# Experts of two routed layers: blocks of 256 slots, two experts' weights per turn, 20 turns in place of 23

## The chip, the cores and the metric

One Trainium2 chip, one core of it. The metric is the device time of one execution in microseconds (us). The kernel is one program for a whole small network: four layers, each an attention and a feed-forward part.

## The reference, cut to what matters

`x` is 32 x 128 tokens of 128 features. Two of the four feed-forward parts are mixtures of 8 experts. Every token goes to its 2 best experts and gets their weighted sum back. Cut to what the change touches:

```python
# layer 1, feed-forward: E = 8 experts, K = 2, hidden F = 256
gate = jnp.sum(jax.nn.one_hot(idx, E) * w[..., None], axis=1)      # 2 of 8 are not zero
hid = jax.nn.silu(jnp.einsum('td,edf->tef', t, w1)) * jnp.einsum('td,edf->tef', t, w3)
y = jnp.einsum('ted,te->td', jnp.einsum('tef,efd->ted', hid, w2), gate)
# layer 2, feed-forward: E = 8, K = 2, hidden DF = 512
h = jax.nn.gelu(jnp.einsum('td,efd->tef', xf, W1) + b1, approximate=False)
y = jnp.einsum('tef,edf->ted', h, W2) + b2
out = jnp.einsum('ted,te->td', y, w)
```

The other parts (three attentions, a scan-like one, two dense feed-forwards) are computed before, between and after, and the change does not edit them.

## The kernel before, in words

The program runs in stages. Layers 0 and 1 share one long stage. Then come the experts of layer 1 (**stage f1**), the attention of layer 2, the experts of layer 2 (**stage f2**), and a tail for layer 3.

`Routes` (L672 on) holds the routing of one mixture. Each token's row is stored twice, once for each of its experts, into a room in DRAM (`self.room`, name `by_expert_r`), by GpSimd's indirect DMAs (L699). The room is cut into blocks of `slots` rows; `LOTS` (L29) says 512. Each expert owns the blocks of its full capacity (4,096 rows), but only its first block is always computed. What overflows is found at run time: `tables` (L772) counts the tokens of each expert and lists the further blocks that hold tokens. `_room` (L63) gives the number of blocks that must be computed so that every token is covered whatever the routing: 8 first blocks and `more` = 15 listed ones, 23 in all. The blocks are zeroed during layer 0, four blocks to a DMA (`clear`, L686, issued at L998 by `cleared`).

`Routes.run` (L804) computes the blocks, one a **turn**:

- `load` (L824): SyncE (SP) issues two DMAs, the expert's weights into `w` (three buffers) and the block's 512 rows into `xt` (three buffers). For the 8 first blocks both addresses are fixed ("static"). For the listed ones SP first reads two registers from the table (L814, "dynamic"). The DMAs of SP are issued in the order in which they stand in its queue, and each waits there until its buffer is free.
- `first` (L841): TensorE turns the rows (four 128x128 transposes into `tpe`), ScalarE or VectorE moves them to `xT`, and `hidden` makes the hidden layer. That is `swiglu` (L1198) in f1: for each of 2 slices of 128 hidden features a matmul with w1 and one with w3 (L1203, L1205), Silu on ScalarE, a product on VectorE. In f2 it is `gelu` (L1378): for each of 4 slices one matmul (L1382) and one Gelu with a bias column of the expert (L1385).
- `second` (L847): 2 (f1) or 4 (f2) accumulating matmuls with w2 (L851) and `finish`, a ScalarE move to `yT` (L1212; L1389 with the bias b2).
- `third` (L856): four transposes back, a VectorE copy to `yt` (L858), and one DMA that stores the block over its old place (L859).

Turns are software pipelined: at turn i the loop at L868 records the load of block i+2, `first` of i+1, `third` of i-1 and `second` of i. A scheduler then orders each engine's instructions by its own estimate, so transposes of the next block and matmuls of the last one interleave. Every f32 matmul is two instructions on TensorE, each with a weight load of its own (PEld), which overlaps the instruction before it.

In f1, GpSimd also clears the key and query stacks of layer 2's attention (L355, L357), and SP loads the first of its keys (L401, 288 KB each) between the block DMAs. After each expert stage the next one gathers the rows back with indirect DMAs (L886).

Of the kernel before, what the change touches and what calls it, by code (L numbers as in the profile page):

```python
# [12 lines left out]
F32 = mybir.dt.float32  # L13
# [3 lines left out]
AF = mybir.ActivationFunctionType  # L17
# [5 lines left out]
P = 128  # L23
NB = 4
E = 8
D = 128
EPS = 1e-5

LOTS = dict(r1=(0, 8, 512), r2=(0, 8, 512))  # L29
MAGIC = 12582912.0  # L30


# [25 lines left out]
E1 = _Cols(w1=256, w3=256, w2=256)  # L58
E2 = _Cols(w1=512, w2=512, b1=4, b2=1)
# [3 lines left out]
def _room(lot):  # L63


    first, end, slots = LOTS[lot]
    cap = (end - first) * NB * P
    more = (2 * cap - E) // slots
    return cap, more, E * cap // slots + more + 1


@with_exitstack
def tile_flamingo_gated(
# [20 lines left out]
    nc = tc.nc  # L94
# [190 lines left out]
    def flat(a):  # L285
        return a.rearrange("p b s -> p (b s)")
# [85 lines left out]
    class Stacks:  # L372
# [13 lines left out]
        def load(self, n, parts, at, group):  # L386

            t = self.slots[n].take()
            heads = slice(0, 9 * self.d)
            for e in range(self.halves):  # L390
                dst = t[heads, 4 * e : 4 * (e + 1)]
                if n == 0:
                    first = (self.H * e + 4 * at) * NB * P
                    src = parts.rearrange("d c h n -> (d c) (h n)")[:, first : first + 4 * NB * P]
                    nc.sync.dma_start(
                        out=dst.rearrange("p m b k -> p (m b k)"),
                        in_=src[:, None, :].to_broadcast([3 * self.d, 3, 4 * NB * P]),
                    )
                else:
                    src = parts.rearrange("(h e) d a (c n) -> e (d a c) h n", e=self.halves, n=NB * P)[e]  # L400
                    nc.sync.dma_start(  # L401
                        out=dst.rearrange("p m b k -> p m (b k)"), in_=src[:, 4 * at : 4 * (at + 1)]
                    )
            if n and self.bias:
                rows = bias_rows[self.bias][:, group * NB * P : (group + 1) * NB * P]
                nc.sync.dma_start(
                    out=t[72:75, 0:4].rearrange("p m b k -> p m (b k)"),
                    in_=rows[:, None, :].to_broadcast([3, 4, NB * P]),
                )
            return t  # L410
# [261 lines left out]
    class Routes:  # L672
# [131 lines left out]
        def run(self, pool, psum, weights, cols, turned, hidden, n_f, finish, spare=1):  # L804

            def static(i):
                block = i * (self.cap // self.slots)
                return slice(block, block + 1), slice(i, i + 1)  # L810

            def dynamic(i):
                vals = [
                    nc.values_load(  # L814
                        table[0:1, k, i : i + 1], engines=[mybir.EngineType.SP], min_val=0, max_val=top,
                        skip_runtime_bounds_check_because="bounded where the table is made",
                    )
                    for k, top in ((1, self.blocks - 1), (0, E - 1))
                ]
                return bass.ds(vals[0], 1), bass.ds(vals[1], 1)  # L820

            n_c = self.slots // P

            def load(i):  # L824
                block, e = static(i) if i < E else dynamic(i - E)
                w = pool.tile([P, cols.n], F32, tag="w", name="w", bufs=3)
                nc.sync.dma_start(out=w, in_=weights[e].rearrange("o p n -> (o p) n"))
                xt = pool.tile([P, n_c, D], F32, tag="xt", name="xt", bufs=2 + spare)
                ins = nc.sync.dma_start(
                    out=xt.rearrange("p c d -> p (c d)"), in_=self.room[block].rearrange("o p n -> (o p) n")  # L830
                )
                self.apart(ins, "tiles", "no two tiles share a block")
                return block, w, xt

            def turn(a):
                tp = psum.tile([P, n_c, P], F32, tag="tp", name="tpe")
                for c in range(n_c):
                    nc.tensor.transpose(tp[:, c, :], a[:, c, :], ident)  # L838
                return tp

            def first(i):  # L841
                block, w, xt = loaded.pop(i)
                xT = pool.tile([P, self.slots], F32, tag="xT", name="xT")
                turned(xT, flat(turn(xt)))
                return block, w, hidden(w, xT)

            def second(block, w, hid):  # L847
                y = psum.tile([P, self.slots], F32, tag="y", name="ye")
                w2 = cols(w, "w2").rearrange("p (f d) -> p f d", d=D)
                for f in range(n_f):  # L850
                    nc.tensor.matmul(y, lhsT=w2[:, f, :], rhs=hid[:, f, :], start=f == 0, stop=f == n_f - 1)  # L851
                yT = pool.tile([P, n_c, P], F32, tag="yT", name="yT", bufs=1 + spare)
                finish(flat(yT), w, y)
                return block, yT

            def third(block, yT):  # L856
                yt = pool.tile([P, n_c, D], F32, tag="yt", name="yt")
                nc.vector.tensor_copy(yt, turn(yT))  # L858
                ins = nc.sync.dma_start(out=self.room[block].rearrange("o p n -> (o p) n"), in_=flat(yt))  # L859
                self.apart(ins, "tiles", "no two tiles share a block")  # L860

            n = E + self.more
            loaded = {0: load(0), 1: load(1)}
            yield
            hid, done = first(0), None
            table = self.tables(pool, psum)
            yield
            for i in range(n):  # L868
                if i + 2 < n:
                    loaded[i + 2] = load(i + 2)  # L870
                after = first(i + 1) if i + 1 < n else None
                if done:
                    third(*done)
                done = second(*hid)
                hid = after
                yield
            third(*done)
            self.done = True

# [308 lines left out]
    with ExitStack() as outer:  # L1188
# [3 lines left out]
        with ExitStack() as stack:  # L1192
            pool, psum = mlp_pools(stack, "f1")

            def turned(xT, tp):
                nc.scalar.mul(xT, tp, COL(col, "g2"))

            def swiglu(w, xT):  # L1198
                hid = pool.tile([P, 2, 512], F32, tag="hid", name="hid", bufs=3)
                for f in range(2):  # L1200
                    fs = slice(f * P, (f + 1) * P)
                    p1 = psum.tile([P, 512], F32, tag="h", name="p1", bufs=3)
                    nc.tensor.matmul(p1, lhsT=E1(w, "w1")[:, fs], rhs=xT, start=True, stop=True)  # L1203
                    p3 = psum.tile([P, 512], F32, tag="h", name="p3", bufs=3)
                    nc.tensor.matmul(p3, lhsT=E1(w, "w3")[:, fs], rhs=xT, start=True, stop=True)  # L1205
                    sil = pool.tile([P, 512], F32, tag="sil", name="sil", bufs=3)
                    nc.scalar.activation(sil, p1, AF.Silu)
                    nc.vector.tensor_tensor(hid[:, f, :], p3, sil, ALU.mult)  # L1208
                return hid

            def finish(yT, w, y):
                nc.scalar.copy(yT, y)  # L1212

            for _ in routes1.run(pool, psum, e1_d, E1, turned, swiglu, 2, finish):
                pass
# [156 lines left out]
        with ExitStack() as stack:  # L1372
            pool, psum = mlp_pools(stack, "f2")

            def turned(xT, tp):
                nc.vector.tensor_scalar(xT, tp, COL(col, "gamma"), COL(col, "beta"), ALU.mult, ALU.add)

            def gelu(w, xT):  # L1378
                hid = pool.tile([P, 4, 512], F32, tag="hid", name="hid", bufs=3)
                for f in range(4):  # L1380
                    ph = psum.tile([P, 512], F32, tag="h", name="ph", bufs=3)
                    nc.tensor.matmul(  # L1382
                        ph, lhsT=E2(w, "w1")[:, f * P : (f + 1) * P], rhs=xT, start=True, stop=True
                    )
                    nc.scalar.activation(hid[:, f, :], ph, AF.Gelu, bias=E2(w, "b1")[:, f : f + 1])  # L1385
                return hid

            def finish(yT, w, y):
                nc.scalar.activation(yT, y, AF.Identity, bias=E2(w, "b2"))  # L1389

            for _ in routes2.run(pool, psum, e2_d, E2, turned, gelu, 4, finish):
                pass
# [236 lines left out]
```

## Time and profile before

| | us |
|---|---|
| median of 3 runs | 2178.75 (2176.64 to 2182.37) |
| the profiled execution, its own time | 2170.34 |
| its span, first to last instruction | 2168.5 |
| stage f1, first weight DMA issued to last store landed | 1261.0 to 1419.7 |
| stage f2, the same | 1781.3 to 1976.7 |
| TensorE busy over the span | 1658.0 (76%) |
| mean granted TensorE clock | 0.860 |
| moved by DMA | 244.66 MB, mean 113 GB/s |

How to read it. A row of a group reads: line, engine, operation, `out<-in`, shapes, count, then busy us and the mean ns of one, then the idle time of the engine ahead of it and who ended it. In the chain of waits each row is start, length and what. In the timeline "SPq" rows are DMAs being issued by SP, not the transfer. Matmuls are pipelined: a row "x2 1.02" is two instructions that overlap, so the spacing is read from start to start.

### The profile page before, as it was taken

The numbers are of one execution on the slowest core, as the hardware profiler recorded it, in microseconds if no ns is written. First come the engines' busy times: TensorE is split into PE (matmuls) and PEld (weight loads), VectorE is DVE, ScalarE is ACT, GpSimd is POOL, SyncE is SP. The second block draws the span as 40 slices with busy tenths as digits, with TensorE's granted clock in tenths as the row PEclk, the third lists the DMA queues.
The fourth block names the chain that finished last, engine by engine and source line by source line (L and its number), as shares of the span: only waits on it lengthen the run. The fifth ranks groups of instructions, "written<-read, shape, count | busy, mean of one in ns | idle before, by whom it ended". The sixth has DMA issues, their size and how long they took to land.

```text
span 2168.5 us, 35498 instructions
## 1 busy us (share of the span) xinstructions
PE 1658.0 (76%) x13624; PEld 1010.3 (47%) x13624; DVE 1197.4 (55%) x3504; ACT 894.0 (41%) x1110; POOL 638.6 (29%) x637
## 2 busy tenths in 40 slices
PE   0599998989999999878777569926666629995355
PEld 0455445456656666555455424414555514442223
DVE  7645446475545476766666433357667631113797
ACT  0376565565787745333323223301111204441244
POOL 5101101020000012454544482056443430003550
PEclk9999999999999999987877779966667759997566
DMA  6564558634332343112212035435344212332110
GB/s 214 154 230 154 187 184 266 219 101 124 105 100 67 94 145 84 51 54 59 56 48 55 25 116 174 141 104 148 110 124 121 71 63 101 135 132 86 41 49 20
DMA packets 164536, 244.66 MB, mean 113 GB/s; under 512 B 20560, under 2 KB 102288, under 8 KB 164112
## 3 DMA queue, kind: packets, MB, share of 16 engines
q1 hardware_dynamic: 156176, 225.62, 34.0%
q0 software_dynamic: 8192, 16.79, 2.7%
q8 instruction: 107, 1.75, 0.4%
q14 instruction: 61, 0.50, 0.1%
HBM read 139.74 MB, written 101.24 MB: 111 GB/s over the span
## 4 chain that ended last, share of the span: by engine, by line
PE 40%; DVE 14%; POOL 13%; issue 8%; ACT 2%; DMA 2%; SPq 0%; POOLq 0%; DVEq 0%; ACTq 0%
PE ye L851 5%; PE ph L1382 4%; PE av L644 4%; POOL by_expert_r L699 4%; PE sct L561 4%; POOL got L886 3%; PE sc L561 3%; PE ph L1037 3%; PE p L1203 2%; PE tpe L838 2%; DVE mx L592 2%; PE p L1205 2%; PE tp L282 1%; POOL r L208 1%; POOL w L249 1%
## 5 line engine op out<-in xcount | busy, mean ns | idle before, releaser
L627 ACT ACTIVATE w<-sct 128x1024 f32<-128x1024 f32 x288 | 292.8, 1024 | 346.4 <-PE sct L561 345.2
L592 DVE TENSOR_REDUCE mx<-sc 128x8 f32<-128x1024 f32 x160 | 194.9, 1220 | 130.0 <-PE sc L561 129.6
L561 PEld LDWEIGHTS <-stack_q 96*128 96x128 bf16 x2560 | 194.4, 110 | 134.5 <-issue 104.3
L886 POOL DMA_INDIRECT got<-by_expert_r,slot_r x128 | 127.7, 998 | 360.8 <-issue 335.0
L597 DVE TENSOR_REDUCE mx<-sc 128x4 f32<-128x1024 f32 x128 | 152.9, 1222 | 132.8 <-PE sc L561 132.3
L644 PE MATMUL av<-w,va 128*9 128x128 f32 (+2 forms) x3584 | 198.1, 295 | 36.7 <-POOL w L630 31.9
L561 PE MATMUL sc<-stack_k,stack_q 96*128 96x128 bf16 x1536 | 145.7, 244 | 46.8 <-DMA stack_k<-k 17.4
L561 PE MATMUL sct<-stack_q,stack_k 128*128 128x128 bf16 (+1 forms) x1536 | 139.5, 236 | 17.3 <-DVE mx L592 8.3
L561 PEld LDWEIGHTS <-stack_k 128*128 128x128 bf16 (+1 forms) x1536 | 111.8, 107 | 69.6 <-issue 66.6
L644 PEld LDWEIGHTS av<-w,va 128*9 128x9 f32 (+2 forms) x3584 | 98.6, 94 | 87.5 <-POOL w L630 43.5
L851 PE MATMUL ye<-hid,w 128*128 128x512 f32 x276 | 133.4, 593 | 2.3 <-DVE hid L1208 2.3
L311 POOL CAST hml<-whole 128x512 bf16<-128x512 f32 (+1 forms) x48 | 30.1, 626 | 343.0 <-ACT whole L310 166.7
L1037 PE MATMUL ph<-h,w 128*128 128x512 f32 x256 | 123.7, 610 | 1.8 <-ACT hn L1040 0.9
L1037 PE MATMUL ph<-hn,w 128*128 128x512 f32 x256 | 121.2, 604 | 0.7 <-ACT hn L1040 0.7
L208 POOL TENSOR_TENSOR r<-r,m 128x4 f32<-128x4 f32 x56 | 58.5, 1044 | 188.8 <-DVE r L207 175.0
L561 PE MATMUL sc<-stack_l,stack_q 96*128 96x128 bf16 x1024 | 110.4, 238 | 0.0
L650 ACT COPY ot<-av 128x512 f32<-128x512 f32 x112 | 65.5, 584 | 99.5 <-PE av L644 96.6
L630 POOL TENSOR_SCALAR_AFFINE_SELECT w<-w 128x1024 f32<-128x1024 f32 x64 | 70.8, 1106 | 113.9 <-ACT w L627 113.7
L561 PE MATMUL sct<-stack_q,stack_l 128*128 128x128 bf16 x1024 | 98.9, 234 | 2.7 <-DVE mx L592 2.7
L627 ACT ACT_TABLE_LOAD x72 | 92.4, 1283 | 9.7 <-PE sct L561 8.5
L699 POOL DMA_INDIRECT by_expert_r<-yn,slot_r x64 | 65.6, 1025 | 83.1 <-DVE slot_r L757 25.4
L656 PE MATMUL tpo<-cst,ot 128*128 128x128 f32 x448 | 82.4, 306 | 9.5 <-ACT ot L650 6.9
(295 smaller groups left out, 3290.5 us busy)
## 6 DMA issues: line engine op xcount, KB each, us to landing
by_expert_r<-zeros SPq DMA_DIRECT2D x40, 1024.0 KB
stack_q<-q SPq DMA_DIRECT2D x96, 288.0 KB
stack_k<-k SPq DMA_DIRECT2D x96, 288.0 KB
k<-hml SPq DMA_DIRECT2D x16, 1152.0 KB
w<-in_e_dram SPq DMA_DIRECT2D x23, 514.5 KB
xt<-by_expert_r SPq DMA_DIRECT2D x46, 256.0 KB
by_expert_r<-yt SPq DMA_DIRECT2D x46, 256.0 KB
q<-hml SPq DMA_DIRECT2D x72, 128.0 KB
```

The source lines that it names most:

```text
L208: nc.gpsimd.tensor_tensor(r, r, m05.to_broadcast([P, NB]), ALU.pow)
L561: nc.tensor.matmul(dst[:, h * P : (h + 1) * P], lhsT=stat[rows, 4 * e + h, b], rhs=mov[rows, 4 * e + h, b], start=start and h == e == 0, s ...
L592: latest["maxima"] = nc.vector.tensor_reduce(mx[:, :, b0 : b0 + 2].rearrange("p h b -> p b h"), sc.rearrange("p i (h k) -> p i h k", h=4), ...
L597: nc.vector.tensor_reduce(mx[:, :, b0], sc.rearrange("p i (h k) -> p h i k", h=4), AX.XY, ALU.max, negate=True,)
L627: latest["weights"] = nc.scalar.activation(w.rearrange("p i h k -> p i (h k)"), sc, AF.Exp)
L644: nc.tensor.matmul(av[32 * h : 32 * h + dv + 1, b * P : (b + 1) * P], lhsT=values[c][:, b, 4 * u + h, :], rhs=w[:, i, h, :], start=c == 0, ...
L656: nc.tensor.transpose(tp[:, b].rearrange("p s r -> p (s r)"), ot[:, b, :], ident)
L699: ins = nc.gpsimd.indirect_dma_start(out=self.rows(), out_offset=bass.IndirectOffsetOnAxis(ap=slots, axis=0), in_=rows, in_offset=None,)
L851: nc.tensor.matmul(y, lhsT=w2[:, f, :], rhs=hid[:, f, :], start=f == 0, stop=f == n_f - 1)
L886: ins = nc.gpsimd.indirect_dma_start(out=got[:, k, b, :], out_offset=None, in_=self.rows(), in_offset=bass.IndirectOffsetOnAxis(ap=self.sl ...
L1037: nc.tensor.matmul(ph, lhsT=wt[:, c, f * P : (f + 1) * P], rhs=h[:, c, :], start=c == 0, stop=c == 3)
L1382: nc.tensor.matmul(ph, lhsT=E2(w, "w1")[:, f * P : (f + 1) * P], rhs=xT, start=True, stop=True)
```

## The change

A block has 256 slots. A turn takes two blocks, the halves of the same 512 columns, each with the weights of its own expert. `_room` then gives `more` = 31, made 32 so that the sum is even: 40 blocks, 20 turns, and 161 blocks of 256 rows in each room in place of 80 of 512. In a turn, `load` issues four DMAs and up to four pairs of register reads, every 512-column matmul becomes two of 256 columns with different weights, `third` stores with two DMAs, and in f2 each Gelu and each move with b2 becomes two of 256 columns, since the bias differs. Silu, the products, the transposes, `xT` in both stages and the copy `yt` keep their shape. The zeroing of the rooms goes in pieces of 8 blocks of 1 KB rows.

```diff
-LOTS = dict(r1=(0, 8, 512), r2=(0, 8, 512))
+LOTS = dict(r1=(0, 8, 256), r2=(0, 8, 256))
+HALVES = slice(0, 256), slice(256, 512)
...
     more = (2 * cap - E) // slots
+    more += (E + more) % 2
     return cap, more, E * cap // slots + more + 1
...
-            def load(i):
-                block, e = static(i) if i < E else dynamic(i - E)
-                w = pool.tile([P, cols.n], F32, tag="w", name="w", bufs=3)
-                nc.sync.dma_start(out=w, in_=weights[e].rearrange("o p n -> (o p) n"))
-                xt = pool.tile([P, n_c, D], F32, tag="xt", name="xt", bufs=2 + spare)
-                ins = nc.sync.dma_start(
-                    out=xt.rearrange("p c d -> p (c d)"), in_=self.room[block].rearrange("o p n -> (o p) n")
-                )
-                self.apart(ins, "tiles", "no two tiles share a block")
-                return block, w, xt
+            def load(u):
+                w = pool.tile([P, 2, cols.n], F32, tag="w", name="w", bufs=3)
+                xt = pool.tile([P, 2 * n_c, D], F32, tag="xt", name="xt", bufs=2 + spare)
+                blocks = []
+                for half in range(2):
+                    i = 2 * u + half
+                    block, e = static(i) if i < E else dynamic(i - E)
+                    nc.sync.dma_start(out=w[:, half], in_=weights[e].rearrange("o p n -> (o p) n"))
+                    ins = nc.sync.dma_start(
+                        out=xt[:, half * n_c : (half + 1) * n_c].rearrange("p c d -> p (c d)"),
+                        in_=self.room[block].rearrange("o p n -> (o p) n"),
+                    )
+                    self.apart(ins, "tiles", "no two tiles share a block")
+                    blocks.append(block)
+                return blocks, [w[:, 0], w[:, 1]], xt
...
-                for f in range(n_f):
-                    nc.tensor.matmul(y, lhsT=w2[:, f, :], rhs=hid[:, f, :], start=f == 0, stop=f == n_f - 1)
+                for w, at in zip(ws, HALVES):
+                    w2 = cols(w, "w2").rearrange("p (f d) -> p f d", d=D)
+                    for f in range(n_f):
+                        nc.tensor.matmul(
+                            y[:, at], lhsT=w2[:, f, :], rhs=hid[:, f, at], start=f == 0, stop=f == n_f - 1
+                        )
...
-                ins = nc.sync.dma_start(out=self.room[block].rearrange("o p n -> (o p) n"), in_=flat(yt))
-                self.apart(ins, "tiles", "no two tiles share a block")
+                for half, block in enumerate(blocks):
+                    ins = nc.sync.dma_start(
+                        out=self.room[block].rearrange("o p n -> (o p) n"),
+                        in_=yt[:, half * n_c : (half + 1) * n_c].rearrange("p c d -> p (c d)"),
+                    )
+                    self.apart(ins, "tiles", "no two tiles share a block")
...
-            n = E + self.more
+            n = (E + self.more) // 2
...
                     p1 = psum.tile([P, 512], F32, tag="h", name="p1", bufs=3)
-                    nc.tensor.matmul(p1, lhsT=E1(w, "w1")[:, fs], rhs=xT, start=True, stop=True)
                     p3 = psum.tile([P, 512], F32, tag="h", name="p3", bufs=3)
-                    nc.tensor.matmul(p3, lhsT=E1(w, "w3")[:, fs], rhs=xT, start=True, stop=True)
+                    for p, name in ((p1, "w1"), (p3, "w3")):
+                        for w, at in zip(ws, HALVES):
+                            nc.tensor.matmul(p[:, at], lhsT=E1(w, name)[:, fs], rhs=xT[:, at], start=True, stop=True)
...
-                    nc.tensor.matmul(
-                        ph, lhsT=E2(w, "w1")[:, f * P : (f + 1) * P], rhs=xT, start=True, stop=True
-                    )
-                    nc.scalar.activation(hid[:, f, :], ph, AF.Gelu, bias=E2(w, "b1")[:, f : f + 1])
+                    for w, at in zip(ws, HALVES):
+                        nc.tensor.matmul(
+                            ph[:, at], lhsT=E2(w, "w1")[:, f * P : (f + 1) * P], rhs=xT[:, at], start=True, stop=True
+                        )
+                    for w, at in zip(ws, HALVES):
+                        nc.scalar.activation(hid[:, f, at], ph[:, at], AF.Gelu, bias=E2(w, "b1")[:, f : f + 1])
...
-            def finish(yT, w, y):
-                nc.scalar.activation(yT, y, AF.Identity, bias=E2(w, "b2"))
+            def finish(yT, ws, y):
+                for w, at in zip(ws, HALVES):
+                    nc.scalar.activation(yT[:, at], y[:, at], AF.Identity, bias=E2(w, "b2"))
```

More of the change, by code (lines that the diff above doesn't have):

```diff
@@ L835, in turn, with first @@
             def turn(a):
-                tp = psum.tile([P, n_c, P], F32, tag="tp", name="tpe")
-                for c in range(n_c):
+                tp = psum.tile([P, 2 * n_c, P], F32, tag="tp", name="tpe")
+                for c in range(2 * n_c):
                     nc.tensor.transpose(tp[:, c, :], a[:, c, :], ident)
                 return tp
-            def first(i):
-                block, w, xt = loaded.pop(i)
-                xT = pool.tile([P, self.slots], F32, tag="xT", name="xT")
+            def first(u):
+                blocks, ws, xt = loaded.pop(u)
+                xT = pool.tile([P, 2 * self.slots], F32, tag="xT", name="xT")
@@ L844, in first @@
                 turned(xT, flat(turn(xt)))
[L845 to L849, printed above, removed]
-                for f in range(n_f):
[L851 to L854, printed above, removed]
@@ L856, in third, with second @@
-            def third(block, yT):
-                yt = pool.tile([P, n_c, D], F32, tag="yt", name="yt")
-                nc.vector.tensor_copy(yt, turn(yT))
-                ins = nc.sync.dma_start(out=self.room[block].rearrange("o p n -> (o p) n"), in_=flat(yt))
-                self.apart(ins, "tiles", "no two tiles share a block")
-            n = E + self.more
+                return blocks, ws, hidden(ws, xT)
+            def second(blocks, ws, hid):
+                y = psum.tile([P, 2 * self.slots], F32, tag="y", name="ye")
+                for w, at in zip(ws, HALVES):
[4 more added lines that the diff above has]
+                        )
+                yT = pool.tile([P, 2 * n_c, P], F32, tag="yT", name="yT", bufs=1 + spare)
+                finish(flat(yT), ws, y)
+                return blocks, yT
@@ new lines, in third @@
+            def third(blocks, yT):
+                yt = pool.tile([P, 2 * n_c, D], F32, tag="yt", name="yt")
+                nc.vector.tensor_copy(yt, turn(yT))
+                for half, block in enumerate(blocks):
[4 more added lines that the diff above has]
+                    self.apart(ins, "tiles", "no two tiles share a block")
@@ L1196, in turned, with swiglu @@
                 nc.scalar.mul(xT, tp, COL(col, "g2"))
-            def swiglu(w, xT):
+            def swiglu(ws, xT):
                 hid = pool.tile([P, 2, 512], F32, tag="hid", name="hid", bufs=3)
@@ L1376, in turned, with gelu @@
                 nc.vector.tensor_scalar(xT, tp, COL(col, "gamma"), COL(col, "beta"), ALU.mult, ALU.add)
-            def gelu(w, xT):
+            def gelu(ws, xT):
                 hid = pool.tile([P, 4, 512], F32, tag="hid", name="hid", bufs=3)
@@ L1381, in gelu, with finish @@
                     ph = psum.tile([P, 512], F32, tag="h", name="ph", bufs=3)
-                    nc.tensor.matmul(
-                        ph, lhsT=E2(w, "w1")[:, f * P : (f + 1) * P], rhs=xT, start=True, stop=True
-                    )
-                    nc.scalar.activation(hid[:, f, :], ph, AF.Gelu, bias=E2(w, "b1")[:, f : f + 1])
-                return hid
-            def finish(yT, w, y):
-                nc.scalar.activation(yT, y, AF.Identity, bias=E2(w, "b2"))
+                    for w, at in zip(ws, HALVES):
[4 more added lines that the diff above has]
+                        nc.scalar.activation(hid[:, f, at], ph[:, at], AF.Gelu, bias=E2(w, "b1")[:, f : f + 1])
+                return hid
+            def finish(yT, ws, y):
+                for w, at in zip(ws, HALVES):
+                    nc.scalar.activation(yT[:, at], y[:, at], AF.Identity, bias=E2(w, "b2"))
             for _ in routes2.run(pool, psum, e2_d, E2, turned, gelu, 4, finish):
```

## The prediction

> **What bounds the kernel now.** I read the chain of waits first, cut to the two expert stages. In f1 and in f2 it repeats with the turn (start, length, what):
>
> ```profile
> 1320.77 1.04 PE p L1203 x2
> 1321.81 0.86 PE p L1205 x2
> 1322.67 0.86 PE p L1203 x2
> 1323.53 0.86 PE p L1205 x2
> 1324.38 0.44 PE tpe L838 x4
> 1324.82 0.86 PE ye L851 x2
> 1325.68 0.44 PE tpe L838 x4
> 1326.12 0.86 PE ye L851 x2
> ...
> 1858.54 3.63 PE ph L1382 x8
> 1862.50 2.58 PE ye L851 x6
> 1865.52 0.86 PE ye L851 x2
> 1866.49 3.63 PE ph L1382 x8
> ```
>
> Only TensorE stands in it. The f2 turn is 1866.49 - 1858.54 = 7.95 us; the f1 turn, from the first p to the next turn's (1326.98 to 1333.24), 6.26 us. Then the table by stretches, one inside each stage (length, PE, PEld, DVE, ACT and POOL busy, granted clock, DMA share, GB/s):
>
> ```profile
> 1320.00:1340.00 20.00, 20.00 (x63) 9.23 (x62) 5.94 (x9) 7.74 (x13) 0.00 (x0) 1.00 0.52 151
> 1860.00:1880.00 20.00, 20.00 (x62) 9.45 (x61) 3.69 (x5) 9.26 (x14) 0.00 (x0) 1.00 0.38 131
> ```
>
> TensorE is busy all the time at the full clock, every other engine under half, the DMA engines 0.52 and 0.38. So a turn is worth its TensorE time, as long as its rows and weights arrive. Of the span, 23 x 6.26 = 144.0 and 23 x 7.95 = 182.9 us are turns.
>
> **TensorE, turn by turn.** An instruction of 512 columns has one weight load (PEld, 190 ns) and starts every 0.43 us: 3.17 us for seven, less the 0.592 us of one, over six gaps. For 256 columns there is no row. From below it takes half, 0.215 us. From above, the nearest row with a load per instruction, in layer 1's projection:
>
> ```profile
> 532.39 0.89 PE L1099 MATMUL po<-wa,oT 128*128 128x128 f32 x6
> 533.12 3.17 PE L1037 MATMUL ph<-h,w 128*128 128x512 f32 x7
> ```
>
> Six of 128 columns in 0.73 us are 0.122 us each, where a quarter of 0.43 is 0.107: the load shows 0.015 us at most. At 256 columns the stream is longer than the load's 0.19 us, so I take 0.216. A turn of f1 then has 24 x 0.216 = 5.18 us of matmuls in place of 12 x 0.43 = 5.16, one of f2 32 x 0.216 = 6.91 in place of 16 x 0.43 = 6.88; the eight transposes stay. A turn hardly grows, and three go: -18.8 in f1, -23.9 in f2, +1.0 for the longer matmuls of 40 turns (+8.4 at 0.015 a piece).
>
> The Trainium skill, "TensorE: Matmul & The Clock Gate", section Back-to-back issue gap, speaks against this: it gives a sustained spacing of 81 ns at 128 columns and 131 ns at 512 and says that both the load and the matmul set it. By it, halving the columns would not halve the time. Row L1099 does not agree for f32 here: a quarter of the columns took 0.28 of the time. An estimate from the page's two figures, 98 ns at 256 columns by a straight line, would make the matmuls of a turn half as long again, 2.6 us more in f1 and 3.4 in f2, and end near 2262. As a mechanism of this kernel it is rival D.
>
> **Fillers.** In f1 the matmuls wait for xT: transposes 0.44 and ScalarE 0.69 us (L1196), with one ye (0.86) in between and a gap of 0.13 us. In the built program's order one half ye and three transposes stand there (0.75 us): +0.1 us a turn, +2 in all; in some turns the four transposes are split and the gap shrinks, so I take +1. In f2 `finish` becomes two moves. A 512-column one took 0.687 us (L1389); the Silu rows of 512 and 1024 columns (0.598, 1.024) give 0.83 ns a column, so 256 columns take 0.47 and the pair 0.95. In the built order the transposes of yT come 0.86 us after the last ye (rows, 0.43, and half a ye, 0.43) and now wait for about 1.2: +0.16 us a turn. The gap ahead of ph (0.10) is filled by more work: -0.10. In all +0.06 x 20 = +1.2. The eight Gelus of a turn take 8 x 0.47 = 3.8 us in place of 2.75, beside 7.9 us of TensorE; the bank of the first is free 0.5 us before the fourth ph wants it, so they stay hidden. If that cover went, each f2 turn would pay up to 1.0.
>
> **Loads.** This is where the change adds: a turn fetches 2 x 384 + 256 KB in f1 (2 x 514.5 + 256 in f2) in place of 384 + 256, with four DMAs, and stores with two. All stand in SP's queue; w waits there until the turn three before is finished, and everything behind it waits too. Two turns of that queue:
>
> ```profile
> 1363.29 0.33 SPq L827 DMA_DIRECT2D w<-in_e_dram  x1
> 1363.87 0.36 SPq L859 DMA_DIRECT2D by_expert_r<-yt  x1
> 1364.75 0.33 SPq L829 DMA_DIRECT2D xt<-by_expert_r  x1
> ...
> 1865.89 0.33 SPq L827 DMA_DIRECT2D w<-in_e_dram  x1
> 1866.72 0.33 SPq L829 DMA_DIRECT2D xt<-by_expert_r  x1
> ```
>
> A dynamic load costs SP 0.83 to 0.88 us (register reads included), a store 0.58. SP is then busy 4 x 0.85 + 2 x 0.58 = 4.6 us a turn, under 6.26. The arrival matters more. The DMA rows of 1363 to 1371 us, in slices of 0.2 us:
>
> ```profile
> DMA  0000002699477999977977510000000000000359
> GB/s 0 0 0 0 0 0 61 169 261 200 184 215 302 364 358 369 394 287 266 297 287 276 215 62 20 0 0 0 0 0 0 0 0 0 0 0 0 46 61 154
> ```
>
> Data flow 0.9 us after the issue, and weights, store and rows (0.92 MB) are through in 3.3 us: 280 GB/s. In f1 after the change, counted from the end of a turn's last ye, the four issues are at 0.2, 1.05, 1.9 and 2.75 us; 1.05 MB at 280 GB/s from 1.1 on end at 4.9. Those rows are wanted after the next turn's transposes, ye, yT, p and ye, 6.0 to 6.2 us. Slack 1.2 us. In f2 the weights come free 1.2 us after the last ye (the later `finish`), 1.31 MB end at 1.2 + 0.9 + 4.7 = 6.8, wanted at 8. So both stay hidden. In f1 four of the eight key loads (288 KB, 1.05 us each at that rate) stand in the built order between later turns' fetches and eat the slack, the others behind the last fetch: 0 to 1 us for each of four turns; I take +1.0, less the 0.9 us that a late xt cost TensorE before (1319.28, next to key loads), so +0.1.
>
> Starts and ends: the first turn needs both halves, 1.05 MB in place of 0.66 MB: +1.2 us a stage, +2.4. The last store is two issues (+0.58 us) of half the bytes (-0.4): +0.4 in all. The table's three operations grow from 120 to 256 elements, +0.1 us each beside TensorE: 0.
>
> Zeroing: 42 DMAs in place of 40, rows of 1 KB in place of 2. No row shows that store; from below 0, from above the rate falls from 340 GB/s to the 290 of the 512-byte loads at 7 to 11 us, 21 us of DMA time for 41 MB. It lies in layer 0, where TensorE is busy 37 of 40 us and the DMA engines 0.5 to 0.8 (140 to 420 us): 0. The scheduler also reorders some of layers 0 and 1: 0 +- 4.
>
> **Sum.** -18.8 - 23.9 + 1.0 + 1.0 + 1.2 + 0.1 + 2.4 + 0.4 = -36.6. The profiled execution took 2170.34 us, span 2168.5 and 1.8 around it: 2134. It was 8.4 us under the median of the runs shown, so the forecast is 2178.75 - 36.6 = 2142.
>
> **The rivals.**
>
> - A, the forecast: 2134 to 2152 (the ends: fillers and starts free and layers 0 and 1 four us better; or +8.4 for the loads on TensorE and the Gelus half hidden).
> - B, f1 becomes bound by transfers. If a row costs the same whether it is 1 or 2 KB (384 rows in 3.3 us now, 768 then), a turn's DMA takes 6.6 us, with a key load 7.6: twenty turns are 136 us, -8 in place of -17: 2151; 7.1 us a turn would make it 2161. For it: the DMA share is 0.52 already. Against: the kernel's first loads, in rows of 512 bytes, run at 290 GB/s. F2 keeps its gain (6.6 under 7.9).
> - C, slower: SP becomes the bound. The first dynamic fetch came 1.88 us after its store (1312.25 to 1314.13). At that price SP needs 4 x 1.88 + 2 x 0.58 = 8.7 us for a turn, more than TensorE in both stages. Sixteen of the twenty turns are dynamic: 16 x 8.7 + 4 x 6.3 = 164 in f1, 16 x 8.7 + 4 x 8 = 171 in f2, +20 and -12, and +3 for starts: 2190. It decides from 1.79 us a fetch on. Against: every later fetch shows 0.85.
> - D, slower: weight loads are not hidden behind 256 columns. A turn has 12 (f1) or 16 (f2) more of them, 560 in all. Wholly exposed they cost 560 x 0.19 = 106 us: 2178.75 - 37.6 + 106 = 2247. It ends slower than before from 0.067 us a load on. Against: 0.015 in row L1099.
> - E, layers 0 and 1 pay for the zeroing or the new order, 5 to 15 us of the 21: about 2152.
>
> **How the numbers follow.** A 0.67, B 0.14, E 0.09, C 0.05, D 0.05. Faster by over 0.3% (6.5 us, about what a measurement of this kernel can tell from no change): A, B and E, 0.90. Within: 0.03 of C, at fetches a little under its price. Slower: D and 0.02 of C, 0.07. The range takes A, B and E and leaves C and D out: 2134 to 2162.
>
> **What would show it.** In the profile after: spacing of 256-column matmuls 0.216 us (D: 0.28 or more); TensorE busy 20 of 20 us and clock 1.00 inside both stages; turns of 6.2 to 6.4 and 7.9 to 8.0 us; f1 some 16 us shorter, f2 some 21; xt as releaser of the transposes only in the first turn and beside the key loads (B, C: in every dynamic turn); DMA share near 0.7 in f1 and 0.6 in f2; layer 2's attention starting 15 to 18 us earlier and all before 1255 us unmoved (E). I am wrong if the rows arrive later than 6.2 us after a turn's last ye in f1, if a dynamic fetch costs SP much more than 0.85 us, or if a load costs TensorE more than 0.067 us.

## The result, and the profile after

The changed kernel takes 2145.0 us, the kernel before 2177.7 in the same comparison: a ratio of 0.985 (95% interval 0.983 to 0.987), 33 us less where 36.6 were forecast. A second comparison, in which both were some 10 us shorter, gave 2133.5 and 2167.8, ratio 0.984 (0.981 to 0.987). The forecast of 2142, its direction and its range held. Not all of its terms did: f1 gained 5 us less than forecast, f2 2 us more. Of the four executions of e7 below, one took 2537.3 us at a mean granted clock of 0.627 where the others have 0.859 to 0.861; no ratio uses it, and without it e7's median is 2124.5.

The stages, from two profiles of each kernel (us). f1 and f2 begin with their first fetch; f1 ends with the next stage's first load, which SP issues behind the last store, and f2 with the issue of its last store.

| | f1 begins | f1 | attention of layer 2 | f2 | tail | span |
|---|---|---|---|---|---|---|
| before | 1261.0 | 158.9 | 361.3 | 193.7 | 193.5 | 2168.5 |
| before, second profile | 1257.9 | 158.8 | 361.5 | 193.8 | 193.3 | 2165.4 |
| after | 1258.8 | 148.1 | 371.9 | 172.0 | 191.7 | 2142.5 |
| after, second profile | 1257.8 | 148.0 | 362.0 | 170.8 | 192.7 | 2131.3 |

Between the two second profiles the 34.1 us lie in f1 (-10.8) and f2 (-23.0), and the rest is -0.3. Of the 10 us that the first profile of after has too much in the attention, 8.2 are one wait, told below (e5).

First the stretches that were shown of before, now of after (length, PE, PEld, DVE, ACT and POOL busy, granted clock, DMA share, GB/s):

```profile
1320.00:1340.00 20.00, 18.72 (x94) 15.39 (x94) 6.04 (x9) 7.21 (x12) 0.00 (x0) 1.00 0.63 190
1860.00:1880.00 20.00, 19.80 (x100) 16.86 (x99) 3.00 (x4) 10.46 (x26) 0.00 (x0) 1.00 0.65 204
```

TensorE is no longer busy all of the 20 us: it lacks 1.3 in f1 and 0.2 in f2. The clock is 1.00 as before, so the throttle has no part in it. The chain of waits of after shows who took the 1.3 us; an f1 turn, then an f2 turn (start, length, what):

```profile
1345.67 0.69 DVE yt L869
1346.37 0.02 issue
1346.38 0.35 SPq L871
...
1346.94 0.36 SPq L871
1347.29 0.04 issue
1347.34 0.27 SPq L817
...
1347.86 0.35 SPq L834
...
1348.76 0.36 SPq L835
...
1349.97 0.34 SPq L834
...
1350.82 3.06 DMA xt<-by_expert_r
1353.88 0.04 issue
1353.93 0.44 PE tpe L846 x2
...
1355.14 3.72 PE p L1221 x16
...
1856.14 0.47 ACT yT L1408
1856.63 0.35 SPq L834
...
1859.17 4.72 DMA xt<-by_expert_r
1863.89 0.04 issue
1863.94 0.44 PE tpe L846 x2
...
1865.68 3.45 PE ph L1399 x16
1869.13 2.60 PE ye L860 x12
```

Before, only TensorE stood here. Now the chain of an f1 turn runs from the copy `yt` through SP's two stores (L871), the register reads (L817), the four fetches (w L834, xt L835) and the landing of the rows, and only then back to the transposes. In some turns of f2 it leaves TensorE too, as here: from the move to `yT`, the last reader of a weight buffer, through the four fetches to the rows. There it costs little; the 20 us of f2 lack 0.2. The same in the list of waits of after, over 1268 to 1400 us, so without the start of the stage (total us, times, longest):

```profile
PEld tpe L846 <- DMA xt<-by_expert_r: 9.1, 13, 1.3
PE tpe L846 <- DMA xt<-by_expert_r: 5.5, 8, 0.9
```

Before, the same view had one such wait, 0.9 us beside the key load. From the first turn's transposes of yT to the eighteenth's (1283.70 to 1398.68) 17 turns take 6.76 us each, where before had 6.26.

The matmuls are as forecast: the sixteen `ph` of an f2 turn take 3.45 us, 0.2156 a piece. In the Trainium skill, "TensorE: Matmul & The Clock Gate", section Back-to-back issue gap, both the load and the matmul set a sustained spacing; the 98 ns estimated from its figures and the larger share of the load that they imply are not what these rows show: 256 columns take half of the 0.43 us of 512.

### The profile page after: what moved, and what is told of

It is laid out like the page before. It is cut to its first block, busy times and chain, and to the rows that moved or that the text cites. A ratio compares the mean times of both kernels' runs of the same rounds, so it can differ in the third digit from the quotient of the medians.

```text
span 2142.5 us, 36779 instructions
## 1 busy us (share of the span) xinstructions
PE 1625.2 (76%) x14046; PEld 1099.8 (51%) x14052; DVE 1189.3 (56%) x3489; ACT 887.5 (41%) x1179; POOL 637.6 (30%) x637
## 4 chain that ended last, share of the span: by engine, by line
PE 35%; DVE 14%; POOL 13%; issue 9%; DMA 4%; ACT 2%; SPq 1%; POOLq 0%; another core or an unknown queue 0%; DVEq 0%; ACTq 0%
POOL by_expert_r L701 4%; PE av L646 4%; PE sct L563 4%; PE ph L1052 4%; PE sc L563 4%; POOL got L901 4%; PE ye L860 3%; PE ph L1399 3%; DMA xt<-by_expert_r 2%; PE p L1221 2%; DVE mx L594 2%; PE tp L284 2%; POOL w L251 1%; PE tpe L846 1%; POOL r L210 1%
## 5 line engine op out<-in xcount | busy, mean ns | idle before, releaser
L563 PEld LDWEIGHTS <-stack_q 96*128 96x128 bf16 x2560 | 193.8, 109 | 137.5 <-issue 106.1
L563 PE MATMUL sct<-stack_q,stack_k 128*128 128x128 bf16 (+1 forms) x1536 | 142.0, 237 | 24.5 <-DVE mx L594 8.8
L860 PE MATMUL ye<-hid,w 128*128 128x256 f32 x480 | 120.7, 380 | 0.1
```

The lines of the kernel that those rows point to most:

```text
L563: nc.tensor.matmul(dst[:, h * P : (h + 1) * P], lhsT=stat[rows, 4 * e + h, b], rhs=mov[rows, 4 * e + h, b], start=start and h == e == 0, s ...
L860: nc.tensor.matmul(y[:, at], lhsT=w2[:, f, :], rhs=hid[:, f, at], start=f == 0, stop=f == n_f - 1)
```

## The experiments

**One stage at a time.** The kernel is written so that a turn takes 512 / slots blocks, and one lot keeps 512.

```diff
-LOTS = dict(r1=(0, 8, 256), r2=(0, 8, 256))
+LOTS = dict(r1=(0, 8, 256), r2=(0, 8, 512))   # e1
+LOTS = dict(r1=(0, 8, 512), r2=(0, 8, 256))   # e2
```

> Only layer 1's experts get blocks of 256 slots and 20 turns; layer 2's keep 23 turns of 512. What the two profiles so far show: stage f1 158.7 us before and 148.1 after, f2 195.4 and 173.3, layer 2's attention 361.6 and 371.9. Theory (the stages' gains are separate, and the 10 us in the attention are one stretch at a low granted clock that belongs to no edit): f1 148, f2 195, the whole about 10.6 us under the kernel before, 2167. Rival (the attention pays for what f1 now does): f1 148, attention 370 to 372, the whole within 3 us of the kernel before.

> Only layer 2's experts get blocks of 256 slots and 20 turns. Theory (separate gains): f1 158.7, attention of layer 2 at 360 to 363, f2 173, the whole 22 us under the kernel before, 2156. Rival (the scatter into a room of 256-slot blocks makes the attention longer): attention 370 to 372, the whole only 12 us under.

Measured: e1 f1 148.5, attention 361.6, f2 194.1; e2 f1 158.4, attention 361.9, f2 171.4. Each stage has its own gain, 10 and 22 us, and neither change lengthens the attention. The times were 2156.0 (ratio 0.992, 0.990 to 0.994) and 2147.3 (0.989, 0.987 to 0.991); the first is 6 us better than the stage explains, while the executions of the kernel before in that comparison range over 8 us (2168 to 2176).

**What the halves cost, and what three turns are worth.** The count of listed blocks is set by hand.

```diff
+MORE = dict(r1=38, r2=38)   # e3: 256 slots, 23 turns
...
+LOTS = dict(r1=(0, 8, 512), r2=(0, 8, 512))   # e4: 512 slots, 20 turns
+MORE = dict(r1=12, r2=12)   # e4
...
+    more = MORE.get(lot, more)   # both
```

> Blocks of 256 slots in both stages, but 38 listed blocks in place of 32, so 23 turns as before: what the halves cost with no turn saved. By the terms of the prediction (1.0 for the matmuls, 2.2 fillers, 0.1 loads, 2.8 starts and ends, each a little more at 23 turns) the sum is 6 to 7 us over the kernel before: 2184. By what the profile after shows (f1 turns of 6.9 us for a predicted 6.3, f2 turns of 7.9) f1 is 148.1 + 3 x 6.9 = 169 and f2 173.3 + 3 x 7.9 = 197, 12 us over: 2190. If weight loads were exposed, 20 us or more over.

> The kernel before with 12 listed blocks of 512 in place of 15: 20 turns in the old form, which leaves out the tokens of blocks beyond the twelfth listed one. It shows what three turns are worth with nothing else changed. Theory: 3 x 6.26 = 18.8 in f1 and 3 x 7.95 = 23.9 in f2, 42.7 us under the kernel before: 2135; f1 140, f2 171.5. Rival (part of a turn is cover for something else that then comes out, such as the zeroed stacks and the key loads in f1): f1 only 8 to 14 us shorter.

Measured: e4 f1 139.9 and f2 170.0, so three turns of the old form are 18.9 and 23.8 us: the largest term of the forecast, to 0.1 us. (In all it was 54 us faster, 2118.3; 10 of these lie in layers 0 and 1, see e12.) e3 took 2183.8, a ratio of 1.006 (1.003 to 1.008), 11.2 us over the kernel before and not the 6 to 7 of the forecast's terms: f1 167.3, f2 196.1. Against e4, the changed kernel's halves cost 8.1 us in f1 (148.0 - 139.9) and 0.8 in f2 (2.0 by the first profile), where the terms said 3.0 and 3.1. The loss is in f1.

**The changed kernel again.** No edit.

> The changed kernel once more, for a second profile of it. In its first profile layer 2's attention took 371.9 us, in the kernel before and in the two kernels with one stage changed 361.4 to 361.9. If the 10 us belong to this program, the attention takes 370 to 373 again and GpSimd waits some 14 us for the slots ahead of the ninth of a run of scatters (4.9 us in the kernel before). If they were chance, the attention takes 361 to 363 and the profiled execution some 10 us less than the 2144 of the first.

Measured: attention 362.0, and the whole 11 us shorter than in the first profile. The 10 us do not belong to the program. GpSimd's scatter behind the wait, in the first profile of after:

```profile
1723.85 0.96 POOL L701 DMA_INDIRECT by_expert_r<-yn,slot_r  x1 [14.35 <-DVE slot_r L759]
```

and in the second:

```profile
1711.57 0.96 POOL L701 DMA_INDIRECT by_expert_r<-yn,slot_r  x1 [6.16 <-DVE slot_r L759]
```

In brackets is the idle time ahead of it: 8.2 us more. The stretches beside it, first profile, then second (granted clock third from the end):

```profile
1710.00:1720.00 10.00, 8.55 (x67) 8.27 (x66) 6.77 (x30) 2.23 (x4) 0.00 (x0) 0.50 0.02 7
```

```profile
1700.00:1710.00 10.00, 8.80 (x126) 7.61 (x125) 7.73 (x35) 3.71 (x5) 4.19 (x5) 0.94 0.12 36
```

The same program ran at a clock of 0.50 where the other execution had 0.94, with half the matmuls in 10 us. A low clock is not peculiar to the first profile (e5 has a mean of 0.55 over 1690 to 1700, just ahead of its stretch); there one more such time fell into the work that the scatter waits for. What made the throttle differ is not shown.

**Late rows: queue order or transfers?** Theory: the rows of f1 are late because their fetch stands in SP's queue behind two stores that wait for `yt`, and behind the weights. Rival: a turn's bytes take that long. Three edits leave the bytes as they are (e8 changes which rows are read, not how many).

```diff
-                w = pool.tile([P, 2, cols.n], F32, tag="w", name="w", bufs=3)
+                w = pool.tile([P, 2, cols.n], F32, tag="w", name="w", bufs=4)    # e6
...
-                    nc.sync.dma_start(out=w[:, half], in_=weights[e].rearrange("o p n -> (o p) n"))
                     ins = nc.sync.dma_start(
                         out=xt[:, half * n_c : (half + 1) * n_c].rearrange("p c d -> p (c d)"),
...
+                    es.append(e)
+                for half, e in enumerate(es):    # e7, behind the loop over both halves
+                    nc.sync.dma_start(out=w[:, half], in_=weights[e].rearrange("o p n -> (o p) n"))
...
-                    block, e = static(i) if i < E else dynamic(i - E)
+                    block, e = static(i)    # e8: block i // E of expert i % E
```

> Four weight buffers in place of three, so that in SP's queue each turn's four fetches stand ahead of the stores of the turn before the one they stood behind. Theory (in f1 the rows are late because their fetch stands behind two stores, which wait for yt): the turns that now average 6.76 us go to the 6.07 of the undelayed ones, 17 x 0.69 = 11.7 us less in f1, which takes 136 to 138; f2 loses its 8.1 to 8.6 us turns, 1 to 2 us less; the whole about 13 us under the changed kernel. Rival (the transfers of a turn, 1.3 MB with the store, fill the time): f1 stays at 146 to 149.

> Only the order of a turn's fetches changes: both halves' rows, then both halves' weights. Theory (the queue): the rows land two issues, 1.7 us, earlier, more than the 1.2 to 1.4 us by which they are late every second turn, and the weights land when the rows land now, which their matmuls, 0.9 us behind the transposes, nearly stand: f1 137 to 141. Rival (transfers): the last byte of a turn lands at the same time, TensorE waits for w in place of xt, f1 146 to 149.

> All 40 blocks at fixed addresses (the first five blocks of each expert), so SP reads no registers: leaves out the blocks that the table would list beyond the fifth. It also frees the order of the fetches, which in the built queue become rows, rows, weights, weights between two pairs of stores. Theory (the queue with its 0.27 us register reads makes the rows late): a fetch costs some 0.4 us in place of 0.85, the rows come over 1.5 us earlier, f1 136 to 139. Rival (transfers): f1 146 to 149 with xt or w as releaser in most turns.

Measured: f1 142.0, 141.6 and 141.7, against 148.0; the times 2126.9 (ratio 0.981 to the kernel before, 0.978 to 0.984), 2125.4 (0.980, 0.977 to 0.983) and 2128.9 (0.980, 0.977 to 0.984). The wait for xt is gone from all three in steady turns. The same stretches as above, in e6:

```profile
1320.00:1340.00 20.00, 19.87 (x103) 16.41 (x102) 6.61 (x11) 7.22 (x13) 0.00 (x0) 1.00 0.68 213
1860.00:1880.00 20.00, 20.00 (x102) 17.26 (x101) 4.06 (x6) 10.71 (x27) 0.00 (x0) 1.00 0.65 204
```

More bytes a second than in after (213 GB/s for 190) and a higher DMA share: the transfers were not the limit. In the chain of e7, a f1 turn is TensorE and its wait for xT again:

```profile
1340.07 0.44 PE tpe L848 x4
1340.51 0.43 PE ye L862 x2
1340.94 0.35 PE tpe L848 x3
1341.30 0.04 issue
1341.34 3.72 PE p L1223 x16
1345.06 0.11 PE tpe L848
1345.17 1.31 PE ye L862 x6
```

Its pieces make 6.39 us a turn, in all three kernels. That is where the numbers of the expectations missed: I had taken 6.07, the interval of the first pair of turns in after, for the undelayed turn, and so hoped for 136 to 141. The rival falls, and the theory of the order holds in this form: in all three the rows of a turn are issued at least a whole turn sooner, behind an earlier pair of stores. What the stores, the weights ahead of the rows and the register reads each cost is not told apart, since e8 also frees the order (its queue has weights, then rows, between two pairs of stores, like e7's, and not rows first as was expected). How e7 does it is seen in SP's rows:

```profile
1340.09 0.92 SPq L873 DMA_DIRECT2D by_expert_r<-yt  x2
1342.12 1.24 SPq L842 DMA_DIRECT2D w<-in_e_dram  x2
1343.85 1.16 SPq L834 DMA_DIRECT2D xt<-by_expert_r  x2
```

Between two pairs of stores SP now issues one turn's weights and the rows of the turn after it: the rows go a turn ahead. In e6 the fourth buffer lets all four fetches go a turn ahead. e7 also starts the stages sooner: from the first fetch to the first p 5.0 us in place of 7.3 and 8.0 in the two profiles of after, and f2 takes 167.2 us where e6 takes 170.6.

The Trainium skill, "Perfetto Trace Analysis", section DMA Optimizations, says that with loops or control flow it may make sense to have one engine issue the inputs and another the outputs. Here stores and loads share SP's queue, and loads issued a turn sooner took the wait away; stores on another queue were not tried, so no run shows what that advice would bring.

**Without late rows, what do the halves cost?** e3 and e7 together.

> 23 turns of two 256-slot blocks (38 listed blocks), with the rows fetched before the weights: the cost of the halves with no turn saved and no late rows. With weights and rows in turn it was 11.3 us over the kernel before (f1 167, f2 196). Theory (late rows are some 7 of these us): f1 is 140.7 + 3 x 6.39 = 160, f2 166.3 + 3 x 7.9 = 190 counted from the first weight fetch, and the whole is 0 to 4 us over the kernel before. Rival (the halves themselves cost it): the whole stays 9 to 12 us over.

Measured: 2174.1, a ratio of 1.001 (1.000 to 1.003), by the ratio 2.6 us over the kernel before (0 to 5.6), as the theory had it; the medians lie 4.9 apart. f1 takes 160.7 and f2 191.2, each 5 to 7 us less than in e3, and against 158.8 and 193.8 before: fed in time, 23 turns of halves cost about what 23 whole ones do. Part of this is the sooner start: from the first fetch to the first ph 4.8 us, where e3 has 8.4 and the kernel before 6.3.

**Both remedies, and the next limit.** e10 has rows first and four buffers of w and xt. e11 has rows first and, in f1:

```diff
-                nc.scalar.mul(xT, tp, COL(col, "g2"))
+                nc.scalar.mul(xT[:, 0:256], tp[:, 0:256], COL(col, "g2"))
+                nc.vector.tensor_scalar(xT[:, 256:512], tp[:, 256:512], COL(col, "g2"), None, ALU.mult)
```

> Rows first, and four buffers each for weights and rows: both remedies at once. Theory (both take away the same wait, and what is left is TensorE's own turn, 6.39 and 7.90 us): no gain over either alone, 2122 to 2128 where they had 2125 and 2127. Rival (each had left part of the wait): f1 turns under 6.39 and 3 us or more under them.

> Rows first, and in f1 the move to xT in two halves of 256 columns, one on ScalarE and one on VectorE. In the undelayed f1 turn of 6.39 us the matmuls and transposes need 24 x 0.2157 + 8 x 0.11 = 6.06; the other 0.33 are the wait for xT (0.25 + 0.70 us after the transposes, with 0.78 us of other work beside it, and the start-up behind it). Theory: a half takes 0.47 us, the wait shrinks by 0.2 to 0.3 us a turn, the turn is 6.1 to 6.2, f1 4 to 6 us shorter than with rows first alone, the whole 2119 to 2122. Rival (the 0.33 us lie elsewhere, or the second half is late instead): turns stay at 6.39.

Measured: e10 2128.9 (0.980, 0.977 to 0.983), f1 turns 6.39 and f1 143.0, no gain over either: both take away the same wait. e11 2125.6 (0.979, 0.976 to 0.982), f1 turns 6.38 and f1 143.2: the expectation missed. The rows of e11 say why:

```profile
1336.26 0.48 ACT L1213 ACTIVATE xT<-tpe,col 128x256 f32<-128x256 f32 x1
1336.44 0.41 PE L848 MATMUL tpe<-cst,yT 128*128 128x128 f32 x2
1336.77 0.48 DVE L1214 TENSOR_SCALAR xT<-tpe,col 128x256 f32<-128x256 f32 x1 [1.15 <-ACT xT L1213]
1336.79 3.81 PE L1224 MATMUL p<-xT,w 128*128 128x256 f32 x16
```

VectorE's half starts when ScalarE's has ended, not beside it: the profile names ScalarE's half as what released it, so in the built program the second write waits for the first. The first p comes sooner, but its group takes longer (3.81 for 3.72), and two transposes of yT stand behind it in place of one.

**The kernel before again.** No edit.

> The kernel before once more, for a second profile of it. Over the kernels so far layers 0 and 1, in which none of the edits changes more than the zeroing, ended between 1250 and 1264 us. If that length belongs to the program (the order the scheduler built), f1 starts at 1260 to 1262 again, and the stages take 158.7, 361 and 194 us; if it is chance from execution to execution, f1 starts 3 us or more away from 1261.

Measured: f1 begins at 1257.9, 3.1 us before the first profile's, and the later stages agree within 0.2. So 3 us of layers 0 and 1 are chance. The other kernels began f1 between 1250.5 (e4) and 1263.6 (e9); whether their built order or chance did that is not settled.

## Why the prediction was right, and where it was not

- **Three turns, -42.7, and +1.0 for longer matmuls**: right. e4 shows -18.9 and -23.8, and the 256-column instruction takes 0.2156 us for a forecast 0.216.
- **Fillers, +1.0 in f1 and +1.2 in f2**: the mechanism was right in f1, the size a little too small. A fed turn takes 6.39 (e6, e7) where 6.26 + 0.02 + 0.05 = 6.33 were forecast. In TensorE's timeline of e7 the last transpose ahead of p starts at 1341.02 and is worth 0.11, and the first p starts at 1341.34: a wait for xT of 0.21 us. Before it was 0.13 (the last ye at 1345.18, worth 0.43, then p at 1345.74), so +0.08 for a forecast +0.05. The first p behind the wait is slow as well, but in both kernels by the same 0.10 us (0.32 to the next start for 0.216; before 0.53 for 0.43). One instruction at a time, the first p of e7, then of before (start, length, what):

```profile
1341.34 0.48 PE L1223 MATMUL p<-xT,w 128*128 128x256 f32 x1
1341.66 0.38 PE L1223 MATMUL p<-xT,w 128*128 128x256 f32 x1
1341.88 0.38 PE L1223 MATMUL p<-xT,w 128*128 128x256 f32 x1
...
1345.74 0.70 PE L1203 MATMUL p<-xT,w 128*128 128x512 f32 x1
1346.27 0.59 PE L1203 MATMUL p<-xT,w 128*128 128x512 f32 x1
```

  In f2 the turn became shorter, 7.90 for 7.95, where the terms made it 8.04: the gap of 0.10 ahead of ph is gone, as forecast, and the delay of the yT pair does not show (its own figures, 1.2 less 0.86, would give 0.34 and not 0.16). Over 20 turns that is 2.6 to 2.8 us, about what f2 gained beyond its terms. The 256-column moves took the 0.47 us that was estimated.
- **Loads, "both stay hidden", +0.1**: this step failed. It measures 6.0 us in f1 (148.0 to 142.0 in e6) and 0.2 in f2 (170.8 to 170.6; 1.4 by the first profile). The forecast counted from the end of a turn's last ye: issues at 0.2 to 2.75, the last rows there at 4.9, wanted at 6.0 to 6.2, so 1.2 us to spare. The turn whose fetches stand in the chain above, in TensorE's timeline of after (start, length, and in brackets the wait):

```profile
1346.70 0.60 PE L860 MATMUL ye<-hid,w 128*128 128x256 f32 x2
1347.14 0.49 PE L846 MATMUL tpe<-cst,yT 128*128 128x128 f32 x3
...
1351.31 1.46 PE L860 MATMUL ye<-hid,w 128*128 128x256 f32 x6
1352.61 0.38 PE L846 MATMUL tpe<-cst,xt 128*128 128x128 f32 x2
1353.93 0.33 PE L846 MATMUL tpe<-cst,xt 128*128 128x128 f32 x1 [0.94 <-DMA xt<-by_expert_r]
```

  The last ye ends at 1347.14, where the next row starts. The issues come at 0.7, 1.6, 2.8 and 3.7: both stores stand ahead of the first, and SP pauses 0.35 us ahead of the third, for which the profile names no cause. The last rows land at 6.7, 3.06 us behind their issue, for a forecast 2.15. They are wanted at 5.85 (1352.99, where the two transposes of the first half end). The slack is -0.9, the wait in the last row. So of the 1.8 us by which these rows land later than forecast, 0.5 lie ahead of the first issue, 0.4 between the issues and 0.9 behind the last one. And a late turn passes it on: late transposes make late p, a late `yt`, a late store, and behind it the next fetch; from the third turn on the turns take 5.85 to 7.50 us, most of them more than the fed 6.39. The prediction had the reason in its own words (everything behind a waiting DMA in SP's queue waits too) but let only w wait, not the stores, and it took the rate of the kernel before, 280 GB/s, for the transfers. In f2 the count was off by as much: the rows of the chain above land at 1863.89, 8.4 us after the last ye of the turn before (1855.50), for a forecast 6.8, and are wanted at 8.1, so the cover of 1.2 us was used up and that turn paid 0.3. There the fetch waits for the move to yT, not for `yt` and the stores; that this is why f2 lost so little is not shown. TensorE busy 20 of 20 us in f1 and an attention 15 to 18 us earlier fell with the loads (18.7, and 10.9 to 13.0 us); a DMA share near 0.7 and 0.6 was about right (0.63 and 0.65).
- **Starts and ends, +2.8**: about right. From the first fetch to the first p 6.05 became 7.33 us, and 8.04 in the second profile; in f2 to the first ph 6.3 became 8.6 and 8.1. Part of that comes back in the next two turns: to the third turn's first p it is +0.3 and +0.8 us, to the third turn's first ph +1.3 and +1.2, for a forecast 1.2 in each stage.
- **Layers 0 and 1, and the zeroing, 0 within 4**: right as far as can be told, 1261.0 and 1257.9 before, 1258.8 and 1257.8 after. E is out.
- **Rivals**: C is out, since later dynamic fetches cost SP 0.85 to 0.9 us, 1.2 with the pause (1347.86, 1348.76, 1349.97), under the 1.79 that it needs. D is out by the spacing. B is out by e6 to e8, but the sign that I gave for it, xt as releaser in every dynamic turn, nearly came (13 waits): the sign does not tell slow transfers from fetches issued late. f1 gained 10.8 us, about what B had (8), for another reason. The upper end of A was reckoned too low: with the 8.4 us of the loads and Gelus half hidden (up to 10) it lies near 2160, not 2152, still inside the range.

That the sum came out so near the forecast was in part luck, because the errors met: by the second profiles f1 gained 5 us less than the 15.8 of its terms, and f2 2 us more than its 20.8; the rest moved by 0.3.

## What to carry to other kernels

Where a buffer's refill is said to be hidden, count from the instruction that stands ahead of it in the issuing queue in the built program, and from what that one waits for, not from the moment when the buffer is free; then close the loop, for lateness that feeds its own next issue came back in most turns here. If a transfer is late while the DMA share is 0.63, move its issue before thinking of bytes: fetching the rows ahead of the weights, with no byte and no buffer more, took 8 us off the changed kernel (2133.5 to 2125.4); the other versions that feed f1 in time and leave nothing out, e6, e10 and e11, stand within 4 us of it, which the intervals do not tell apart. And compare stages of two profiles of the same kernel before explaining a stage that was not edited.

## What the runs showed of the hardware that was not expected

- One and the same program lost 8 us in a single wait of one execution, where the granted clock was 0.50 in place of 0.94 over 10 us, and not in the next.
- A wait of TensorE for ScalarE costs 0.10 us more than the wait: the first matmul behind it takes that much longer to the next start, with 256 columns (0.32 us for 0.216) as with 512 (0.53 for 0.43).
- Rows of 1 KB, beside the 3 KB rows of the weights, did not hold the transfers back: with them the DMA engines moved 213 GB/s over 20 us at a share of 0.68 (e6), before 151 at 0.52.
